# A linear-attention layer and six windowed transformer layers: v's projection moved within the slot, both sums of squares behind the division, mask matmuls on 32 rows

## The chip, the cores and the metric

The kernel runs on one core of one Trainium2 chip. The metric is the device time of one execution in microseconds (us). Before the change it is 3887.95 us, the median of three runs (3886.12 to 3890.18). In the text TensorE is the matrix engine (PE in the profile; PEld are its weight loads), VectorE is DVE, ScalarE is ACT, GpSimd is POOL, and SyncE (SP) issues the DMAs.

## What is computed

The input is 8 sequences of 512 tokens with 128 features. Two sublayers follow each other, each between two layer norms with a residual:

```
x = x + layernorm(linear_attention(layernorm(x)))
x = x + layernorm(stack(layernorm(x)))
```

The first is attention with a Taylor expansion of the exponential in place of the softmax. The second, where the change lies, is a stack of six layers. Each has local attention with 16 heads of 64 and a gated feed-forward part with GELU:

```
qkv = x @ Wqkv; q, k, v = split(qkv)             # x has half its features shifted by a token
q = l2norm(q) * qs;  k = l2norm(k) * ksc         # per head
q, k = rotary(q) * scale, rotary(k) / scale
sim  = q . k * 8     # a window of 32 queries sees 64 keys: its own window and the one before
sim  = where(mask, -big, sim);  attn = softmax(sim)
x = (attn @ v) @ Wo + x
x = (a * gelu(gate)) @ W2 + b2 + x,  [a, gate] = layernorm(shift(x)) @ W1 + b1
```

The mask of a window depends on places within the window alone: the same 32 x 64 pattern for each of the four windows of a block of 128 tokens, save the first window of a sequence, which has no window before it.

## The kernel before

The first sublayer runs by itself in the first 540 us or so. The stack then runs in *slots*, one turn of the loop at L703. A unit is one block of 128 tokens of one sequence in one layer; there are 6 x 8 x 4 = 192. They run through the loop as a pipeline: in slot t, `at(t, lag, step)` runs a step for unit t-lag. TensorE's order is written out by hand (`manual_schedule`, L694): it executes its instructions as the loop issues them. The other engines' orders come from a planner, which ranks instructions by a simulated time and by `high_priority`, and keeps to edges laid with `issue_behind`. Each engine executes in order.

In a slot TensorE's order is:

- `proj` 0 (unit t): q's projection, L421, four passes of 128x512 into PSUM tag "mm"
- `out_project` (t-3), L603, after which VectorE adds to `state` (L608)
- `proj` 1: k's projection
- `by_keys` (t-2): eight transposes of the exponentials into two banks of tag "tr", each emptied by ScalarE (L564, tile pT)
- `values` (t): v's projection, L481, into tag "mm"; ScalarE copies it to v0 (L482, in two banks at once); ten DMAs on SP (L489, L490, L492), or for the first block of a sequence eight and two memsets on GpSimd (L487), spread it by windows into v2
- `by_features` 0 (t-1): eight transposes of q and k, two banks of "tr", emptied by ScalarE (L514, tiles qT and kT)
- `weigh_values` (t-2), L574: 64x32 tiles of the array, into tag "s"; VectorE divides by the sums (L582, the division; tile on)
- `by_features` 4 (t-1): the other eight transposes, two banks of "tr"
- once in four slots each, for a whole sequence: `feed_norm` (transposes nx, L616), `feed_first` (transposes xn, L641), `feed_middle` (three chunks of L625 and L626 with GELU), `feed_last` (L657)
- `scores` (t-1): two mask matmuls (L527) start the two banks of "s" with the mask, and 64x32 tiles (L534) add the products; VectorE takes the maxima (L542), ScalarE the exponentials (L546)
- `out_by_features` (t-2): eight transposes, two banks of "tr", emptied by ScalarE (L596)

PSUM has eight banks, and all are used: "mm" has two buffers of two banks, "tr" two of one bank, "s" one of two banks. A buffer is written again when all who read its last tile are done. So the users of "mm" in a slot take turns: `proj` 0 and `values` have the same buffer, `proj` 1 the other, then the feed-forward steps.

In `proj`, VectorE multiplies the projection by the rotary tables (two L429, one L436), ScalarE squares it (two L444, tile sq), and GpSimd adds (L454). `sum_squares` is VectorE's reduction of sq (L457). For q (s=0) it is issued within `proj`; for k (s=1) after `weigh_values`, with an edge behind the last division. `unit_length` then makes the inverse root on ScalarE (L95, L97) and multiplies on GpSimd (L470). In slots with GELU it stands behind `feed_middle`, and ScalarE loads another activation table at the slot's start (L82) and back (L76).

Of the kernel before, what the change touches and what calls it, by code (L numbers as in the profile page):

```python
# [9 lines left out]
BF16 = mybir.dt.bfloat16  # L10
AF = mybir.ActivationFunctionType
ALU = mybir.AluOpType
AX = mybir.AxisListType
# [7 lines left out]
W = 32  # L21
NEG = -(2.0**100)
EPS = 1e-5


@with_exitstack
def sandwich_kernel(ctx: ExitStack, tc: tile.TileContext, ins: dict, out: bass.AP):
# [38 lines left out]
    mask = const.tile([P, 2 * W], BF16, tag="mask", name="mask")  # L66
    mask0 = const.tile([P, 2 * W], BF16, tag="mask0", name="mask0")

    def transposed(ps, src, rows, cols):
        nc.tensor.transpose(ps[:cols, :rows], src, ident[:rows, :rows])  # L70


    tables, exps, divisions = [], [], []

    def log_and_exp(behind):
        ld = nc.scalar.preload_act_table_set("natural_log_exp_and_others")  # L76
# [332 lines left out]
    def proj(u, s):  # L409

        L, b, j = u["L"], u["b"], u["j"]
        wqkv, tab = L["wqkv"], L["tab"]
        lhs = state[b][:, j * P : (j + 1) * P]
        if s == 0:
            u["ss"] = f2.tile([P, 2, H], F32, tag="ss", name="ss")
            u["qk"] = f2.tile([P, 2, H, 2, HF], F32, tag="qk", name="qk")
        ss, qk = u["ss"], u["qk"]

        ps = psum.tile([P, 2, H, HF], F32, tag="mm", name="mm")
        for a in range(2):  # L420
            nc.tensor.matmul(  # L421
                ps[:, a].rearrange("p h d -> p (h d)"), lhs, wqkv[:, s, a, :], start=True, stop=True
            )
        sq = f2.tile([P, H, 2, HF], F32, tag="sq", name="sq")
        t1 = f2.tile([P, 2, H, HF], F32, tag="t1", name="t1")
        t2 = f2.tile([P, 2, H, HF], F32, tag="t2", name="t2")

        def turned(a):
            nc.vector.tensor_tensor(  # L429
                t2[:, a], ps[:, 1 - a],  # L430
                tab[:, 2 * s + 1, j, HF * a : HF * (a + 1)].unsqueeze(1).to_broadcast([P, H, HF]),
                ALU.mult,
            )

        def straight():
            nc.vector.tensor_tensor(  # L436
                t1, ps,
                tab[:, 2 * s, j, :].rearrange("p (a d) -> p a d", a=2).unsqueeze(2)
                .to_broadcast([P, 2, H, HF]),
                ALU.mult,  # L440
            )

        def squared(a):
            nc.scalar.activation(sq[:, :, a, :], ps[:, a], AF.Square)  # L444

        turned(0)
        turned(1)
        straight()
        squared(0)
        squared(1)  # L450
        u["sq"] = sq
        if s == 0:
            sum_squares(u, 0)
        nc.gpsimd.tensor_tensor(qk[:, s].rearrange("p h a d -> p a h d"), t1, t2, ALU.add)  # L454

    def sum_squares(u, s):
        su = nc.vector.tensor_reduce(  # L457
            u["ss"][:, s], u["sq"].rearrange("p h a d -> p h (a d)"), AX.X, ALU.add
        )
        if s == 1 and divisions:  # L460
            issue_behind(su, divisions[-1])

    def unit_length(u):
# [10 lines left out]
    def values(u):  # L474
        L, b, j = u["L"], u["b"], u["j"]
        lhs = state[b][:, j * P : (j + 1) * P]

        v0 = f3.tile([P, 2, 512], F32, tag="v0", name="v0")
        ps = psum.tile([P, 2, 512], F32, tag="mm", name="mm")
        for p in range(2):  # L480
            nc.tensor.matmul(ps[:, p, :], lhs, L["wqkv"][:, 2, p, :], start=True, stop=True)  # L481
        nc.scalar.copy(v0, ps)  # L482

        v2 = f2.tile([P, 4, 512], F32, tag="v2", name="v2")
        for p in range(2):
            if j == 0:
                nc.gpsimd.memset(v2[HD * p : HD * p + W, 0, :], 0.0)  # L487
            else:
                nc.sync.dma_start(v2[HD * p : HD * p + W, 0, :], u["B"]["v0"][P - W : P, p, :])  # L489
            nc.sync.dma_start(v2[HD * p + W : HD * (p + 1), 0, :], v0[0:W, p, :])  # L490
            for w in range(1, 4):
                nc.sync.dma_start(  # L492
                    v2[HD * p : HD * (p + 1), w, :], v0[W * (w - 1) : W * (w + 1), p, :]
                )
        u["B"]["v0"] = v0
        u["v2"] = v2

    def by_features(u, c):

        j, qk, B_ = u["j"], u["qk"], u["B"]  # L500
        if c == 0:
            u["qT"] = f1.tile([P, NP, P], F32, tag="qT", name="qT")
            if j == 0:
                B_["kT"] = f2.tile([P, NP, W + P], F32, tag="kT", name="kT")
                nc.gpsimd.memset(B_["kT"][:, :, :W], 0.0)
            u["kT"] = B_["kT"]
        for s in range(2):
            ps = psum.tile([P, 4, P], F32, tag="tr", name="tr")
            for i in range(4):
                h0 = 2 * (c + i)  # L510
                transposed(ps[:, i, :], qk[:, s, h0 : h0 + 2].rearrange("p h a d -> p (h a d)"), P, P)
            dst = u["qT"][:, c : c + 4, :] if s == 0 else u["kT"][:, c : c + 4, W:]
            with tc.high_priority():
                nc.scalar.copy(dst, ps)  # L514
        if c == NP - 4 and j < NB - 1:
            B_["kT"] = f2.tile([P, NP, W + P], F32, tag="kT", name="kT")
            nc.gpsimd.tensor_copy(B_["kT"][:, :, :W], u["kT"][:, :, P:])

    def scores(u):

        qT, kT = u["qT"], u["kT"]


        mk = mask0 if u["j"] == 0 else mask
        sp = psum.tile([P, 2, NP, 2 * W], F32, tag="s", name="sp", bufs=1)
        for p in range(2):
            nc.tensor.matmul(  # L527
                sp[:, p], identb, mk.unsqueeze(1).to_broadcast([P, NP, 2 * W]),
                start=True, stop=False, skip_group_check=True,
            )  # L530
        for pair in range(NP):
            for w in range(4):
                for p in range(2):
                    nc.tensor.matmul(  # L534
                        sp[W * w : W * (w + 1), p, pair, :],
                        qT[HD * p : HD * (p + 1), pair, W * w : W * (w + 1)],
                        kT[HD * p : HD * (p + 1), pair, W * w : W * (w + 2)],
                        start=False, stop=True, skip_group_check=True,
                    )
        mx = f2.tile([P, 2, NP], F32, tag="mx", name="mx")  # L540
        with tc.high_priority():
            nc.vector.tensor_reduce(mx, sp, AX.X, ALU.max, negate=True)  # L542
        pe = f2.tile([P, NP, 2, 2 * W], F32, tag="pe", name="pe")
        for pair in range(NP):
            for p in range(2):
                ex = nc.scalar.activation(  # L546
                    pe[:, pair, p, :], sp[:, p, pair, :], AF.Exp, bias=mx[:, p, pair : pair + 1]
                )
                issue_behind(ex, tables[-1])
        exps.append(ex)  # L550
        su = f2.tile([P, NP, 2], F32, tag="su", name="su")
        nc.vector.tensor_reduce(su, pe, AX.X, ALU.add)
        nc.vector.reciprocal(su, su)
        u["pe"], u["su"] = pe, su
# [133 lines left out]
    def at(t, lag, step, *args, ends=False):  # L688
        if 0 <= t - lag < len(units) and (not ends or units[t - lag]["j"] == NB - 1):
            step(units[t - lag], *args)  # L690
# [3 lines left out]
    with tc.manual_schedule(engines={mybir.EngineType.PE}):  # L694
# [8 lines left out]
        for t in range(len(units) + 7):  # L703
            if t < len(units):
                u = units[t]
                if u["l"] not in layers:
                    layers[u["l"]] = load_layer(u["l"])
                u["L"] = layers[u["l"]]


            gelus = 0 <= t - 5 < len(units) and units[t - 5]["j"] == NB - 1
            if gelus:
                gelu_only()
            at(t, 0, proj, 0)
            at(t, 3, out_project)
            at(t, 0, proj, 1)
            at(t, 2, by_keys)

            if t == 0:
                head_norm(NG - 1)  # L720
            at(t, 0, values)
            if t == 1:
                attn_out(B - 1)
            if t == 3:
                to_state(B - 1)
            at(t, 1, by_features, 0)
            at(t, 2, weigh_values)
            at(t, 0, sum_squares, 1)
            if not gelus:
                at(t, 0, unit_length)  # L730
            at(t, 1, by_features, 4)
            at(t, 3, feed_norm, ends=True)
            at(t, 4, feed_first, ends=True)
            at(t, 5, feed_middle, ends=True)
            if gelus:
                at(t, 0, unit_length)
            at(t, 6, feed_last, ends=True)
            at(t, 1, scores)
            at(t, 2, out_by_features)

# [90 lines left out]
```

## Time and profile before

The profile is of one execution of 3893.85 us, whose span from first to last instruction is 3892.1 us; TensorE's granted clock was 0.99 of full speed in it.

| | |
|---|---|
| median of three runs | 3887.95 us |
| profiled execution | 3893.85 us, span 3892.1 us |
| slots 1503.63 to 1520.32, to 1535.01, to 1551.53, to 1571.3 us | 16.69, 14.69, 16.52, 19.8 us |
| TensorE busy between 1000 and 2000 us | 969.0 us |
| the same for VectorE, ScalarE, GpSimd | 763.6, 714.2, 554.4 us |
| data moved | 233.46 MB, mean 60 GB/s |

How to read it: a line of the groups names the source line, the engine, the operation, output and inputs by the program's tiles, the shape, and the count; after the bar come busy time in us and the mean of one in ns; after the second bar the engine's idle time just before these instructions, and who ended it. In the timeline the columns are start and length in us, then engine, line, operation; instructions of one kind in a row are merged, with their count. Matmuls are pipelined: lengths overlap, and the time that a step takes is the distance from its start to the next one's start. An f32 matmul appears as two passes, a transpose as one.

### The profile page before, as it was taken

To read this page: it belongs to the slowest core of one execution; us is meant where nothing else is said; L and a number is where in the kernel's file an instruction comes from. 1 tells how busy PE (TensorE), PEld (TensorE's weight loads), DVE (VectorE), ACT (ScalarE), POOL (GpSimd) and SP (SyncE) were. 2 spreads that over 40 slices of the span, in tenths; PEclk is the share of its full clock that TensorE was granted. 3 is DMA by queue.
4 is the path that set the end of the run, shared out by engine and by line. 5 is a ranking of instruction groups with operands and counts; after the bars stand their busy time and mean duration, and the time that the engine had idled before them with its cause. 6 is when DMAs were issued, how large, how long until landed. Compare 5 with 4: busy or idle time off the path is not lost.

```text
span 3892.1 us, 149565 instructions
## 1 busy us (share of the span) xinstructions
PE 3729.8 (96%) x65600; PEld 2474.2 (64%) x65600; DVE 2818.2 (72%) x4300; ACT 2657.5 (68%) x6745; POOL 1837.0 (47%) x1311
## 2 busy tenths in 40 slices
PE   8999989999999999999999999999999999999997
PEld 4555456666666666666666666666666666666665
DVE  4555567777867777777777777777787777777775
ACT  5565656776767777777777677777677777766664
POOL 0000025555555555555555555555555555555552
PEclk9999999999999999999999999999999999999998
DMA  2000012222222222222222322223222222222221
GB/s 81 17 9 12 6 50 71 59 66 60 76 74 63 63 63 66 71 75 65 60 62 64 82 65 66 65 56 82 70 66 59 66 65 56 65 68 68 64 67 37
DMA packets 153208, 233.46 MB, mean 60 GB/s; under 512 B 32622, under 2 KB 53356, under 8 KB 151788
## 3 DMA queue, kind: packets, MB, share of 16 engines
q1 hardware_dynamic: 152556, 223.89, 22.4%
q8 instruction: 517, 8.47, 0.9%
q14 instruction: 135, 1.11, 0.1%
HBM read 24.54 MB, written 4.19 MB: 7 GB/s over the span
## 4 chain that ended last, share of the span: by engine, by line
PE 89%; ACT 5%; issue 3%; DVE 2%; DMA 0%; POOL 0%; POOLq 0%; DVEq 0%; SPq 0%; ACTq 0%
PE tr L70 17%; PE mm L421 17%; PE mm L481 9%; PE py L603 9%; PE sp L534 7%; PE po L574 6%; PE y L282 4%; PE mm L625 3%; PE py L657 3%; PE mm L626 3%; PE sc L252 2%; PE sp L527 2%; ACT sq L444 2%; PE vv L230 2%; PE po L318 2%
## 5 line engine op out<-in xcount | busy, mean ns | idle before, releaser
L454 POOL TENSOR_TENSOR qk<-t,t 128x1024 f32<-128x1024 f32 x384 | 909.2, 2368 | 999.6 <-DVE t L436 999.5
L421 PE MATMUL mm<-wqkv,state 128*128 128x512 f32 x1536 | 727.1, 596 | 3.7 <-ACT v L482 2.6
L470 POOL TENSOR_TENSOR qk<-qk,ss 128x1024 f32<-128x1024 f32 x384 | 722.3, 1902 | 16.0
L429 DVE TENSOR_TENSOR t<-mm,tab 128x512 f32<-128x512 f32 x768 | 497.8, 685 | 242.8 <-PE mm L421 231.3
L546 ACT ACTIVATE pe<-sp,mx 128x64 f32<-128x64 f32 x3072 | 651.4, 376 | 27.6 <-DVE mx L542 27.3
L436 DVE TENSOR_TENSOR t<-mm,tab 128x1024 f32<-128x1024 f32 x384 | 465.9, 1213 | 0.0
L457 DVE TENSOR_REDUCE ss<-sq 128x16 f32<-128x1024 f32 x384 | 461.9, 1203 | 2.0 <-ACT sq L444 2.0
L444 ACT ACTIVATE sq<-mm 128x512 f32<-128x512 f32 x768 | 422.6, 610 | 47.2 <-DVE t L436 45.6
L603 PEld LDWEIGHTS py<-oT,wo 128*128 128x128 f32 x3072 | 374.8, 193 | 93.5 <-issue 56.2
L70 PEld LDWEIGHTS tr<-ident,qk 128*128 128x128 f32 x3072 | 345.7, 141 | 127.1 <-issue 105.7
L70 PE MATMUL tr<-ident,qk 128*128 128x128 f32 x3072 | 412.1, 277 | 7.4 <-ACT qT L514 2.3
L596 ACT COPY oT<-tr 128x512 f32<-128x512 f32 x384 | 207.3, 589 | 266.2 <-PE tr L70 265.2
L421 PEld LDWEIGHTS mm<-wqkv,state 128*128 128x128 f32 x1536 | 264.1, 192 | 191.6 <-issue 188.0
L481 PE MATMUL mm<-wqkv,state 128*128 128x512 f32 x768 | 367.9, 602 | 16.8 <-ACT sq L444 16.8
L603 PE MATMUL py<-oT,wo 128*128 128x128 f32 x3072 | 376.0, 276 | 1.0 <-ACT oT L596 0.9
L582 DVE TENSOR_TENSOR on<-po,su 128x1024 f32<-128x1024 f32 x192 | 235.1, 1224 | 170.1 <-PE po L574 170.1
L534 PEld LDWEIGHTS sp<-kT,qT 64*32 64x32 f32 x24576 | 271.9, 106 | 116.7 <-issue 113.8
L574 PE MATMUL po<-v,pT 64*32 64x64 f32 x24576 | 299.3, 225 | 44.7 <-issue 44.7
L482 ACT COPY v<-mm 128x1024 f32<-128x1024 f32 x192 | 194.5, 1013 | 211.0 <-PE mm L481 211.0
L534 PE MATMUL sp<-kT,qT 64*32 64x64 f32 x24576 | 312.2, 227 | 26.0 <-issue 25.2
L574 PEld LDWEIGHTS po<-v,pT 64*32 64x32 f32 x24576 | 258.5, 105 | 86.4 <-issue 86.2
L542 DVE TENSOR_REDUCE mx<-sp 128x16 f32<-128x1024 f32 x192 | 234.6, 1222 | 106.9 <-PE sp L534 106.3
(108 smaller groups left out, 5171.0 us busy)
## 6 DMA issues: line engine op xcount, KB each, us to landing
v<-v SPq DMA_DIRECT2D x1152, 128.0 KB
v<-v SPq DMA_DIRECT2D x672, 64.0 KB
wqkv<-in_L_ffn_Wqkv_dram SPq DMA_DIRECT2D x6, 1536.0 KB
wo<-in_L_ffn_Wo_dram SPq DMA_DIRECT2D x6, 512.0 KB
xin<-_attn_hidden_states_dram SPq DMA_DIRECT2D x8, 256.0 KB
xr<-_attn_hidden_states_dram SPq DMA_DIRECT2D x8, 256.0 KB
x<-xr SPq DMA_DIRECT2D x8, 256.0 KB
xr<-x SPq DMA_DIRECT2D x8, 256.0 KB
```

Source lines behind the costliest of these rows:

```text
L70: nc.tensor.transpose(ps[:cols, :rows], src, ident[:rows, :rows])
L421: nc.tensor.matmul(ps[:, a].rearrange("p h d -> p (h d)"), lhs, wqkv[:, s, a, :], start=True, stop=True)
L429: nc.vector.tensor_tensor(t2[:, a], ps[:, 1 - a], tab[:, 2 * s + 1, j, HF * a : HF * (a + 1)].unsqueeze(1).to_broadcast([P, H, HF]), ALU.mult,
L436: nc.vector.tensor_tensor(t1, ps, tab[:, 2 * s, j, :].rearrange("p (a d) -> p a d", a=2).unsqueeze(2) .to_broadcast([P, 2, H, HF]), ALU.mult,)
L444: nc.scalar.activation(sq[:, :, a, :], ps[:, a], AF.Square)
L454: nc.gpsimd.tensor_tensor(qk[:, s].rearrange("p h a d -> p a h d"), t1, t2, ALU.add)
L470: nc.gpsimd.tensor_tensor(t, t, ss[:, i, :].unsqueeze(2).to_broadcast([P, H, HD]), ALU.mult)
L481: nc.tensor.matmul(ps[:, p, :], lhs, L["wqkv"][:, 2, p, :], start=True, stop=True)
L534: nc.tensor.matmul(sp[W * w : W * (w + 1), p, pair, :], qT[HD * p : HD * (p + 1), pair, W * w : W * (w + 1)], kT[HD * p : HD * (p + 1), pa ...
L546: ex = nc.scalar.activation(pe[:, pair, p, :], sp[:, p, pair, :], AF.Exp, bias=mx[:, p, pair : pair + 1])
L574: nc.tensor.matmul(po[W * w : W * (w + 1), p, pair, :], pT[r, pair, W * w : W * (w + 1)], v2[r, w, HD * pair : HD * (pair + 1)], start=Tru ...
L603: nc.tensor.matmul(py, L["wo"][:, c, :], oT[:, c, :], start=(c == 0), stop=(c == NP - 1))
```

## The change

Four things change.

1. `values` is split. Its matmuls stay in `values`, which moves from before `by_features` 0 to after `weigh_values`. The copy of v and all that follows it, the DMAs and memsets of v2 too, become `spread`, called after `by_features` 4, with an edge that puts the copy behind the last copy of q's and k's transposes.
2. q's sum of squares leaves `proj` and is issued beside k's, after `weigh_values`; both have the edge behind the last division. The tile sq is kept for each.
3. The mask matmuls of all blocks but a sequence's first take 32 rows: the stationary operand is a new constant `each` (64 x 128, four 32 x 32 identities side by side in each half), the moving one the mask's first 32 rows for p=0 and the next 32 for p=1. The first block of a sequence keeps the 128-row identity and `mask0`.
4. `each` is made once, at the start, by eight small casts on VectorE.

```diff
+    each = const.tile([2 * W, P], BF16, tag="each", name="each")
+    for a in range(2):
+        for w in range(4):
+            nc.vector.tensor_copy(
+                each[W * a : W * (a + 1), W * w : W * (w + 1)], ident[W * a : W * (a + 1), W * a : W * (a + 1)]
+            )
...
-        u["sq"] = sq
-        if s == 0:
-            sum_squares(u, 0)
+        u["sq", s] = sq
...
-            u["ss"][:, s], u["sq"].rearrange("p h a d -> p h (a d)"), AX.X, ALU.add
+            u["ss"][:, s], u["sq", s].rearrange("p h a d -> p h (a d)"), AX.X, ALU.add
         )
-        if s == 1 and divisions:
+        if divisions:
             issue_behind(su, divisions[-1])
...
             nc.tensor.matmul(ps[:, p, :], lhs, L["wqkv"][:, 2, p, :], start=True, stop=True)
-        nc.scalar.copy(v0, ps)
+        u["v0"], u["v0ps"] = v0, ps
+
+    def spread(u):
+        j, v0 = u["j"], u["v0"]
+        cp = nc.scalar.copy(v0, u.pop("v0ps"))
+        if copies:
+            issue_behind(cp, copies[-1])
...
-                nc.scalar.copy(dst, ps)
+                copies.append(nc.scalar.copy(dst, ps))
...
-        mk = mask0 if u["j"] == 0 else mask
...
         for p in range(2):
+            r = slice(W * p, W * (p + 1))
+            lhs, mk = (identb, mask0) if u["j"] == 0 else (each[r], mask[r])
             nc.tensor.matmul(
-                sp[:, p], identb, mk.unsqueeze(1).to_broadcast([P, NP, 2 * W]),
+                sp[:, p], lhs, mk.unsqueeze(1).to_broadcast([lhs.shape[0], NP, 2 * W]),
                 start=True, stop=False, skip_group_check=True,
             )
...
+            at(t, 1, by_features, 0)
+            at(t, 2, weigh_values)
             at(t, 0, values)
...
-            at(t, 1, by_features, 0)
-            at(t, 2, weigh_values)
+            at(t, 0, sum_squares, 0)
             at(t, 0, sum_squares, 1)
             if not gelus:
                 at(t, 0, unit_length)
             at(t, 1, by_features, 4)
+            at(t, 0, spread)
```

More of the change, by code (lines that the diff above doesn't have):

```diff
@@ L67, in sandwich_kernel @@
     mask0 = const.tile([P, 2 * W], BF16, tag="mask0", name="mask0")
+    each = const.tile([2 * W, P], BF16, tag="each", name="each")
[4 more added lines that the diff above has]
+            )
     def transposed(ps, src, rows, cols):
         nc.tensor.transpose(ps[:cols, :rows], src, ident[:rows, :rows])
-    tables, exps, divisions = [], [], []
+    tables, exps, divisions, copies = [], [], [], []
     def log_and_exp(behind):
```

## The prediction

> **What bounds the kernel now.** I read the busy shares, then the chain of waits, the groups by line and shape, and the timeline of single instructions on TensorE and ScalarE.
>
> ```profile
> PE 3729.8 (96%) x65600; PEld 2474.2 (64%) x65600; DVE 2818.2 (72%) x4300; ACT 2657.5 (68%) x6745; POOL 1837.0 (47%) x1311
> PE 89%; ACT 5%; issue 3%; DVE 2%; DMA 0%; POOL 0%; POOLq 0%; DVEq 0%; SPq 0%; ACTq 0%
> L481 PE MATMUL mm<-wqkv,state 128*128 128x512 f32 x768 | 367.9, 602 | 16.8 <-ACT sq L444 16.8
> L70 PE MATMUL tr<-ident,xn 128*128 128x128 f32 x192 | 32.2, 290 | 14.4 <-ACT qT L514 11.9 <-DVE xn L115 2.5
> L574 PE MATMUL po<-v,pT 64*32 64x64 f32 x24576 | 299.3, 225 | 44.7 <-issue 44.7
> ```
>
> TensorE is the limit: what it doesn't wait for costs nothing. The change can save 16.8 us of visible waiting before v's projection (L481). The second TensorE row is a wait that two transposing steps in a row already pay. The third is instruction supply, which stops long runs of small matmuls.
>
> Now one slot (one block of 128 tokens through the loop at L703; 192 of them). Columns: start, length, engine, line.
>
> ```profile
> 1525.54 1.04 PE L70 MATMUL tr<-ident,pe 128*128 128x128 f32 x8
> 1526.18 1.08 ACT L564 COPY pT<-tr 128x512 f32<-128x512 f32 x2 [0.27 <-PE tr L70]
> 1526.41 1.88 PE L481 MATMUL mm<-wqkv,state 128*128 128x512 f32 x4
> 1528.13 1.04 PE L70 MATMUL tr<-ident,qk 128*128 128x128 f32 x8
> 1529.10 1.48 PE L574 MATMUL po<-v,pT 64*32 64x64 f32 x128
> 1530.52 1.09 PE L70 MATMUL tr<-ident,qk 128*128 128x128 f32 x8
> 1531.45 0.60 PE L70 MATMUL nx<-ident,state 128*128 128x128 f32 x4
> 1531.90 0.59 PE L527 MATMUL sp<-mask,identb 128*128 128x512 bf16 x2
> ```
>
> Read from start to start, for the lengths overlap. Eight transposes (two PSUM banks of tag "tr", which has just two) take 0.87 us, v's projection 1.72, and nothing lies between. The two copies that empty the banks run 1526.18 to 1527.26, **under v's projection**. That cover is what the change takes away.
>
> **The price of the lost cover.** After it, by_features(0) follows by_keys at once, and its first bank is by_keys' first. The trace has this case once in four slots: feed_first after by_features(4).
>
> ```profile
> 1546.75 1.09 PE L70 MATMUL tr<-ident,qk 128*128 128x128 f32 x8
> 1547.45 0.58 ACT L514 COPY qT<-tr 128x512 f32<-128x512 f32 x1 [1.37 <-PE tr L70]
> 1547.93 0.59 ACT L514 COPY kT<-tr 128x512 f32<-128x512 f32 x1
> 1548.09 0.66 PE L70 MATMUL tr<-ident,xn 128*128 128x128 f32 x4 [0.24 <-ACT qT L514]
> 1548.58 0.59 PE L527 MATMUL sp<-mask,identb 128*128 128x512 bf16 x2
> ```
>
> From 1546.75 to 1548.09 it takes 1.34 us where by_features(4) takes 0.93 (1530.52 to 1531.45): 0.41 to 0.42 us of waiting, and xn's four transposes take 0.49 instead of nx's 0.45 (the next weights weren't loaded ahead; single starts say 0.055). So **0.475 us**. The copies themselves say the same: by_keys starts at 0, its first copy at 0.64 and ends at 1.23, with 0.06 to the next matmul 1.29, against 0.87. The second copy ends at 1.72, when the first bank has just been refilled (1.29+0.055+0.436=1.78), so the second bank adds nothing to 0.05. In the 144 slots without GELU: 144 x 0.475 = 68.4 us.
>
> In the 48 slots with GELU the table load makes the squares late, and v waits:
>
> ```profile
> 1556.76 1.04 PE L70 MATMUL tr<-ident,pe 128*128 128x128 f32 x8
> 1556.96 1.09 ACT L444 ACTIVATE sq<-mm 128x512 f32<-128x512 f32 x2
> 1557.93 1.08 ACT L564 COPY pT<-tr 128x512 f32<-128x512 f32 x2
> 1558.10 1.98 PE L481 MATMUL mm<-wqkv,state 128*128 128x512 f32 x4 [0.31 <-ACT sq L444]
> ```
>
> by_keys ends at 1557.63. v now waits 0.47 us and loses 0.10 of weight load (1.82 instead of 1.72): 0.57, which goes. In its place by_features(0) waits for the first pT copy, 1558.52+0.06, so 0.95, plus 0.055: 1.01. Net +0.44, x 48 = 21 us. **The wait saved is smaller than the wait that takes its place.** Together +89 us; bounds 0.42 x 192 = 81 and 0.53 x 192 = 102.
>
> **v's projection after the small tiles.** A step that follows another tiling of the array can't load its first weights ahead.
>
> ```profile
> 310.54 1.98 PE L303 MATMUL ms<-ysq,same 128*128 128x512 f32 x4
> 312.45 1.51 PE L282 MATMUL y<-am,tv 128*64 128x384 f32 x8
> ```
>
> Four f32 matmuls between two other tilings take 1.91 us against v's 1.72: 0.19, of which 0.09 is the exit (transposes before L574 take 0.97 against 0.87), so 0.10 the entry; transposes there pay 0.06 (0.93 against 0.87). by_features(4) is freed of 0.06, v pays 0.10: +0.046 x 192 = +9 us (0 to 20).
>
> **Mask matmuls.** Two bf16 matmuls, 0.216 us each by their starts, in 144 slots (blocks with j=0 keep the full identity). On rows 0-31 and 32-63 they may run together, as L252's four row groups do (sixteen passes of 256 columns in 0.87 us, as long as four). But 128 to 32 rows is one more change of tiling: 0.09, and the first weights exposed: 0.10 for loads that last 192 ns, 0.06 for 141 ns, so about 0.02 for L527's 98 ns, an estimate from these rows. The later change to 64x32 is paid already. 0.216-0.007-0.09-0.02 = 0.10, x 144 = **-14 us**. Bounds: -31 (no change paid) and +16 (no overlap, change paid). The Trainium skill, "TensorEngine Tiling (Array Packing)", Key Properties, says that a change of tiling mode drains the engine; "TensorE: Matmul & The Clock Gate", Part 3, has packed matmuls start some 4 ns apart. By the second page alone this part would save 31 us; the 0.09 us rows side with the first.
>
> **v's copy behind q's and k's.** ScalarE's copy (1.01 us) moves to after by_features(4): from its start S, qT and kT copies run to S+1.72, v's to S+2.73. The bank pair is wanted again by feed_middle's second chunk in GELU slots, at S+0.87+1.72=S+2.59; with 0.06 it starts at 2.79: +0.2, some of it taken back at the third chunk: 0.17 x 48 = **+8 us** (0 to 12). Elsewhere the pair's next user comes over 4 us after S. Queued behind the copy on ScalarE: GELU (ready S+2.8), unit_length, the exponentials (S+3.5 or later). The ten DMAs on SP and the memset on GpSimd of v2 start some 3 us later; v2 is read two slots on, some 25 us away, and SP spent 7 to 8 us on them.
>
> **Sums of squares behind the division.** Both reductions (1.20 us each) now queue after L582. k's rotation comes 1.2 us sooner; the division needs L574, which ends 1.2 us sooner too. From the slot's start (1520.32 for the one shown) the sums end at 12.65 us today (1532.97); then at 8.96 (end of L574: 6.09 for by_keys, 0.4 wait, 1.0, 1.4) + 0.2 + 1.22 + 2 x 1.2 = 12.8. The mask waits for the division alone, which now has v's 1.72 us as cover, but it waited only 0.6 us in all. Behind them on VectorE: layer norm, then the score maxima, ready later still. 0 us; if the maxima slipped by 1 us in the slots with layer norm, the exponentials have some 0.7 us of slack (end 1539.92, wanted by the second bank at 1540.67), so 0.3 x 48 = 14. Eight small casts for `each` at the start lie in VectorE's idle 3.4 us before x lands: 0 (at most 1.5).
>
> **Instruction supply.** Blocks of L574 and L534 take 1.41 us at best; over that they add 58 and 52 us in all, mostly stops for instructions. The new order shifts where a fetch falls: v's 1.72 us leaves the stretch before L574 and enters the one before L534. 0, with -30 to +30.
>
> **Sum.** 89+9-14+8 = +92 us. The profiled execution took 3893.85 us (span 3892.1), 5.9 over the median: 3887.95+92 = **3980 us**.
>
> **The rivals.**
> 1. *Faster: the banks come free in time.* If by_keys' copies kept pace with its transposes, so that by_features(0) didn't wait, the wait of v would simply go: -0.57 x 48 = -27, with -14+9+8 -24, so 3864. It decides if the first copy ends within 0.87 us of by_keys' start; today 1.23. For it: ScalarE is 68% busy; against: it idles before this copy, so it can't be earlier. Chance 0.09 (0.07 below -0.2%, 0.02 within).
> 2. *Supply gets worse.* L574 is reached 1.72-0.475 us sooner while the fetch comes when it did: 62 stops grow by up to 1.25: +78, so 4058. Against: in the records of the instruction queue these fetches start about 0.5 us before L574, whatever went before. 0.08.
> 3. *The mask doesn't overlap* (the change doesn't do what it says): +16 for -14, so 4010. Against: L252. 0.11.
> 4. *ScalarE puts pT's copies ahead of the squares in GELU slots:* their 0.57 us stays saved, -27, so 3953. 0.12.
>
> The forecast keeps 0.60. Range 3930 to 4030: it takes in 3, 4 and the bounds of supply, and leaves 1 and 2 out (0.17). Faster by over 0.2% (about what this measurement tells from none) 0.07, same 0.02, slower 0.91.
>
> **What would show it.** TensorE's transposes of qk with an idle time of tens of us put down to ScalarE's pT copy (today none), by_keys to by_features(0) 1.29 us from start to start; L481's wait for sq gone, its block 1.82; L527 to L534 0.42 instead of 0.52; L625 with a wait for v's copy. If by_keys to by_features(0) stays 0.87, the prediction falls.

## The result, and the profile after

The changed kernel takes **4027.03 us** (median; 4021.14 to 4030.63), beside 3889.06 us for the kernel before (3886.12 to 3890.41): a ratio of **1.0354, with a 95% interval from 1.0336 to 1.0372**. It is slower by 138 us; the forecast was slower by 92, with the range up to 4030. The profiled execution took 4021.14 us with a span of 4019.4 us at a granted clock of 0.989.

The busy shares, the engines of the chain of waits, then five TensorE groups by line and shape, and last the two groups of the kernel before (transposes of q and k, scores) that weren't shown yet:

```profile
PE 3758.1 (93%) x65600; PEld 2464.0 (61%) x65600; DVE 2815.7 (70%) x4308; ACT 2666.0 (66%) x6745; POOL 1840.5 (46%) x1311
PE 78%; ACT 9%; DVE 5%; issue 4%; POOL 2%; DMA 1%; SPq 0%; ACTq 0%; POOLq 0%; DVEq 0%
```

```profile
L76 PE MATMUL tr<-ident,qk 128*128 128x128 f32 x3072 | 419.8, 278 | 102.9 <-ACT pT L576 82.6 <-POOL qk L458 18.6 <-ACT qT L524 1.4
...
L485 PE MATMUL mm<-wqkv,state 128*128 128x512 f32 x768 | 391.8, 632 | 6.5 <-issue 4.9 <-ACT sq L450 1.4
...
L546 PE MATMUL sp<-kT,qT 64*32 64x64 f32 x24576 | 304.8, 226 | 12.2 <-issue 12.1
...
L586 PE MATMUL po<-v,pT 64*32 64x64 f32 x24576 | 295.3, 226 | 75.6 <-issue 75.6
...
L76 PE MATMUL tr<-ident,xn 128*128 128x128 f32 x192 | 32.3, 289 | 13.5 <-ACT qT L524 11.0 <-DVE xn L121 2.5
```

```profile
L70 PE MATMUL tr<-ident,qk 128*128 128x128 f32 x3072 | 412.1, 277 | 7.4 <-ACT qT L514 2.3 <-issue 2.2 <-ACT pT L564 1.2
...
L534 PE MATMUL sp<-kT,qT 64*32 64x64 f32 x24576 | 312.2, 227 | 26.0 <-issue 25.2
```

TensorE's busy time rose by 28 us, and it went from 96% of the span to 93%: most of the loss is waiting. The transposes of q and k waited 7.4 us before and now wait 102.9: 82.6 of it is put down to ScalarE's copy of pT, 18.6 to GpSimd's qk (wrongly, where it was looked at; see the slots with `feed_first`). v's projection (L485, L481 before) lost its 16.8 us of waiting for the squares, but its busy time rose by 24 us. The idle time "issue" of the weighing matmuls (L586, L574 before) rose from 44.7 to 75.6 us, that of the scores (L546, L534 before) fell from 26.0 to 12.2. xn's transposes wait as they did.

One slot without GELU, from the timeline (start, length, engine, line):

```profile
1627.26 1.04 PE L76 MATMUL tr<-ident,pe 128*128 128x128 f32 x8
...
1627.90 1.08 ACT L576 COPY pT<-tr 128x512 f32<-128x512 f32 x2 [0.27 <-PE tr L76]
...
1628.63 1.12 PE L76 MATMUL tr<-ident,qk 128*128 128x128 f32 x8 [0.33 <-ACT pT L576]
1629.68 1.48 PE L586 MATMUL po<-v,pT 64*32 64x64 f32 x128
1631.09 1.98 PE L485 MATMUL mm<-wqkv,state 128*128 128x512 f32 x4
```

From 1627.26 to 1628.63 `by_keys` takes 1.37 us where it took 0.87: the first pT copy (0.586 us) ends at 1628.49, and `by_features` 0 starts 0.144 us behind it. That block takes 1.05 us (0.97 before). The projection of v comes straight after the small tiles.

From the single starts I took, for 45 slots of each of the four kinds (with `feed_norm`, `feed_first`, `feed_middle`, `feed_last`), the mean distance from each step's start to the next. A slot went from 17.164 to 17.879 us; times 192 that is 137 us, as much as the medians differ. (The two profiled executions differ by 127 us in their spans: outside the slots where all steps run, the changed kernel's was some 9 us shorter.)

| step, start to next start | before, us | after, us | difference x 192 |
|---|---|---|---|
| `by_keys` | 0.984 | 1.569 | +112 |
| `by_features` 0 | 0.967 | 1.050 | +16 |
| v's projection | 1.746 | 1.892 (half of the slots at 1.821) | +28, of which +14 without stops |
| `weigh_values` | 1.719 | 1.877 | +30 |
| `by_features` 4 (with what it waits in `feed_first`) | 1.042 | 0.989 | -10 |
| masks, and what the step ahead of them pays | | | -17 |
| `feed_middle`, second chunk | | | +5 |
| `scores` | 1.685 | 1.575 | -21 |
| `out_by_features`, `proj` 0 | 2.737 | 2.701 | -7 |

### The profile page after: what moved, and what is told of

The parts are those of the page before. It is cut to its first block, busy times and chain, and to the rows that moved or that the text cites. A ratio compares the mean times of both kernels' runs of the same rounds, so it can differ in the third digit from the quotient of the medians.

```text
span 4019.4 us, 149714 instructions
## 1 busy us (share of the span) xinstructions
PE 3758.1 (93%) x65600; PEld 2464.0 (61%) x65600; DVE 2815.7 (70%) x4308; ACT 2666.0 (66%) x6745; POOL 1840.5 (46%) x1311
## 4 chain that ended last, share of the span: by engine, by line
PE 78%; ACT 9%; DVE 5%; issue 4%; POOL 2%; DMA 1%; SPq 0%; ACTq 0%; POOLq 0%; DVEq 0%
PE tr L76 15%; PE mm L427 13%; PE mm L485 9%; PE po L586 7%; PE py L615 7%; PE sp L546 6%; PE y L288 4%; PE mm L637 3%; PE mm L638 3%; PE py L669 3%; PE sc L258 2%; ACT pT L576 2%; POOL qk L458 2%; ACT sq L450 2%; PE vv L236 2%
## 5 line engine op out<-in xcount | busy, mean ns | idle before, releaser
L427 PE MATMUL mm<-wqkv,state 128*128 128x512 f32 x1536 | 728.5, 598 | 2.9 <-ACT v L490 2.6
L524 ACT COPY qT<-tr 128x512 f32<-128x512 f32 x384 | 224.8, 585 | 509.3 <-PE tr L76 504.8
L76 PE MATMUL tr<-ident,qk 128*128 128x128 f32 x3072 | 419.8, 278 | 102.9 <-ACT pT L576 82.6
L461 DVE TENSOR_REDUCE ss<-sq 128x16 f32<-128x1024 f32 x384 | 448.5, 1209 | 0.7 <-ACT sq L450 0.6
L485 PE MATMUL mm<-wqkv,state 128*128 128x512 f32 x768 | 391.8, 632 | 6.5 <-issue 4.9
L586 PE MATMUL po<-v,pT 64*32 64x64 f32 x24576 | 295.3, 226 | 75.6 <-issue 75.6
L586 PEld LDWEIGHTS po<-v,pT 64*32 64x32 f32 x24576 | 257.4, 105 | 108.4 <-issue 107.9
L546 PE MATMUL sp<-kT,qT 64*32 64x64 f32 x24576 | 304.8, 226 | 12.2 <-issue 12.1
L546 PEld LDWEIGHTS sp<-kT,qT 64*32 64x32 f32 x24576 | 269.6, 105 | 68.2 <-issue 66.4
```

The source lines that it names most:

```text
L427: nc.tensor.matmul(ps[:, a].rearrange("p h d -> p (h d)"), lhs, wqkv[:, s, a, :], start=True, stop=True)
L546: nc.tensor.matmul(sp[W * w : W * (w + 1), p, pair, :], qT[HD * p : HD * (p + 1), pair, W * w : W * (w + 1)], kT[HD * p : HD * (p + 1), pa ...
L586: nc.tensor.matmul(po[W * w : W * (w + 1), p, pair, :], pT[r, pair, W * w : W * (w + 1)], v2[r, w, HD * pair : HD * (pair + 1)], start=Tru ...
```

## The experiments

The theory: v's projection covered the two pT copies, and without that cover `by_features` 0 waits for its bank. Rival A: the other parts (sums, copy, masks) cost the time. Rival B: the supply of instructions does. Each ratio is to the kernel before, timed on the same chip (median there 3898.15 to 3905.7 us). The runs went to four chips, so ratios of two runs are told apart only where their intervals are. Steps and idle times are compared with the one trace of the kernel before, an execution of 3893.85 us, 4 to 12 us below these medians, so a sum of steps can come out that much higher than the ratio.

### The move alone, and the change without it

The kernel before with v's whole step behind `weigh_values`:

```diff
+            at(t, 1, by_features, 0)
+            at(t, 2, weigh_values)
             at(t, 0, values)
...
-            at(t, 1, by_features, 0)
-            at(t, 2, weigh_values)
```

> The kernel before, with v's projection (its copy and DMAs with it) moved behind weigh_values and nothing else. Theory 'cover' (by_features 0 waits for by_keys' two PSUM banks): by_keys to by_features 0 takes 1.37 us from start to start in slots without GELU and 1.9 with it, as in the changed kernel, and the time is 4030 us (4005 to 4055), since the mask's 16 us aren't saved and v's early copy stands ahead of q's and k's second pair. Rival 'sums' (VectorE's order with both reductions behind the division delays the maxima and all that follows): within 20 us of the kernel before. Rival 'late copy' (v's copy and its DMAs being late): within 20 us of the kernel before.

Measured: 4052.07 us, ratio 1.0384 (1.037 to 1.0398).

The changed kernel with that move undone, all else kept:

```diff
             at(t, 0, values)
...
+            at(t, 1, by_features, 0)
+            at(t, 2, weigh_values)
             at(t, 0, sum_squares, 0)
```

> The changed kernel with v's matmuls put back between by_keys and by_features 0; copy late, sums behind the division and 32-row mask stay. Theory 'cover': the 136 us go, 3889 - 16 (mask) + 5 (feed_middle waits for v's copy) + 12 (squares late in slots after a layer norm) = 3890 us (3875 to 3905). Rival 'sums' and rival 'late copy': stays at 4000 us or more.

Measured: 3909.36 us, ratio 1.0023 (1.0014 to 1.0032).

The move alone costs at least as much as the whole change (the intervals just touch), and all the rest costs 0.2% (in it v waits 26.3 us for the squares in slots with GELU, 16.8 before). Two groups of the move alone:

```profile
L70 PE MATMUL tr<-ident,qk 128*128 128x128 f32 x3072 | 419.6, 278 | 95.5 <-ACT pT L564 89.9 <-POOL qk L470 2.8 <-ACT qT L514 1.8
L70 PE MATMUL tr<-ident,xn 128*128 128x128 f32 x192 | 32.3, 289 | 33.7 <-ACT qT L514 31.3 <-DVE xn L115 2.5
```

The first row is the wait of the changed kernel. The second, 14.4 us in the kernel before, is the price of v's copy left in `values`: ScalarE does it ahead of the qT copy, and in slots with `feed_first` `by_features` 4 takes 1.74 us (1.36 before, 1.30 after the full change). So the late copy, forecast as a loss of 8 us, takes back 0.44 x 48 = 21 us here. Rival A falls as the main cause.

### The other parts, each alone

The kernel before with q's sum behind the division:

```diff
-        if s == 0:
-            sum_squares(u, 0)
...
+            at(t, 0, sum_squares, 0)
             at(t, 0, sum_squares, 1)
```

> The kernel before with q's sum of squares behind the division. Theory 'cover' gives it a small part: in slots after one with layer norm the maxima come 0.4 us later, so the exponentials, so q's squares; v's matmuls wait some 0.25 us there: +12 us, 3901 (3889 to 3910). Rival 'sums': +60 us or more.

Measured: 3902.63 us, ratio 0.9999 (0.9991 to 1.0008). The expected 12 us aren't there.

With the masks of 32 rows alone (the constant `each`, and the lines of `scores` as in the change):

> The kernel before with the 32-row mask matmuls alone. Theory: two row groups run together, one change of tiling is added: 0.11 us a slot in 144 slots, -16 us, 3873 (3865 to 3880). Rival without a price for the change of tiling: -31 us, 3858. Rival without overlap: +15 us, 3904.

Measured: 3891.02 us, ratio 0.997 (0.9961 to 0.9979): 10.6 us instead of 16. Its steps show why. In a slot with `feed_norm` the mask block goes from 0.522 to 0.318 us and nx's transposes ahead of it from 0.455 to 0.533, as forecast; but the scores behind it go from 1.807 to 1.966 us. They are reached sooner, and stop longer for instructions. How much of the 0.16 us is due to that isn't sharply shown: two kernels without these masks, the load alone and the late copy alone (below), have 1.92 and 1.90 us there.

With v's copy behind the copies of q and k alone:

```diff
-        nc.scalar.copy(v0, ps)
+        u["v0"], u["v0ps"] = v0, ps
...
             at(t, 1, by_features, 4)
+            at(t, 0, spread)
```

> The kernel before with v's copy and its DMAs issued behind q's and k's second copies, all else as before. From the run with v put back (+8 us with the mask's -11 and the sums' 0 in it) this part is left with +18 us: feed_middle's second chunk waits some 0.1 us for the copy in GELU slots (+5), and the scores there take 1.67 instead of 1.42 us, while v's DMAs run (+12): 0.45% slower (0.3 to 0.6). Rival 'copy is free' (the predicted +8 and nothing in the scores): 0.2%.

Measured: 3910.8 us, ratio 1.0016 (1.0005 to 1.0026), less than expected. The scores in slots with GELU did go from 1.416 to 1.618 us, as expected. Of idle time, the weighing matmuls' fell from 44.7 to 41.2 us, but the scores' rose from 26.0 to 29.3, so what makes the time fall short of the expected 18 us stays open.

The changed kernel with q's sum back in `proj`:

```diff
+        if s == 0:
+            sum_squares(u, 0)
...
-            at(t, 0, sum_squares, 0)
```

> The changed kernel with q's sum of squares back in proj. Alone, this part measured nothing; together with the lost cover it should: in slots after a layer norm q's squares end 0.4 us later and push pT's copies, for which by_features 0 now waits (1.64 instead of 1.37 us). Theory: 13 us and some of the GELU slots' wait come back, 12 to 20 us below the changed kernel, ratio to before 1.031 (1.029 to 1.033), and by_keys to by_features 0 is 1.37 in these slots. Rival 'sums are free in any company': 1.0354 as the changed kernel.

Measured: 4033.99 us, ratio 1.0338 (1.0322 to 1.0354): no clear difference from the changed kernel's 1.0354, so the moved sum is worth little in either.

### Half of the cover

The changed kernel with v's first matmul between `by_keys` and `by_features` 0, the second behind `weigh_values`:

```diff
+            at(t, 0, values, 0)
             at(t, 1, by_features, 0)
             at(t, 2, weigh_values)
-            at(t, 0, values)
+            at(t, 0, values, 1)
```

> The changed kernel with v's first matmul (0.86 us) between by_keys and by_features 0 and the second behind weigh_values. Theory 'cover': 0.86 us is more than the wait of 0.49, so the wait goes as a whole and not by half, and by_features 0 takes 0.97 again; left are the late copy, the first weights behind weigh_values (+9) and some of the instruction supply (0 to 15), less the mask: ratio 1.006 (1.003 to 1.010). Rival 'it is the place of v itself, behind the small tiles' (supply and first weights): about half of the loss stays, 1.018.

Measured: 3922.5 us, ratio 1.0053 (1.0041 to 1.0066). Three groups of it:

```profile
L76 PE MATMUL tr<-ident,qk 128*128 128x128 f32 x3072 | 410.0, 277 | 6.4 <-issue 3.6 <-ACT qT L523 1.4 <-ACT pT L575 1.2
L485 PE MATMUL mm<-wqkv,state 128*128 128x512 f32 x768 | 430.2, 642 | 21.0 <-ACT sq L450 17.1 <-issue 3.9
L585 PE MATMUL po<-v,pT 64*32 64x64 f32 x24576 | 295.6, 225 | 78.8 <-issue 78.8
```

Half of v's projection (0.86 us) covers the wait of 0.49 us **whole**: 82.6 us put down to pT became 1.2. Half of the cover hid all of the wait, not half of it. The wait for the squares is back in slots with GELU.

### The same wait, with v in another place

Rival B needs a kernel with the wait but another order of long and short instructions. Here `values` and `by_features` 0 of the kernel before change places, and v stays ahead of `weigh_values`:

```diff
+            at(t, 1, by_features, 0)
             at(t, 0, values)
...
-            at(t, 1, by_features, 0)
             at(t, 2, weigh_values)
```

> The kernel before with v's projection and by_features 0 exchanged: by_keys, by_features 0, values, weigh_values. The cover is gone, but v stays ahead of the small tiles, so instruction supply and first weights are as before. Theory 'cover': 0.49 us of wait in 144 slots and 0.59 in 48 (99 us), 0.08 for weights loaded late in by_features 0 (15), 5 less for v: +109 us, ratio 1.028 (1.025 to 1.031), against 1.038 for the move alone; L574 then stops for some 45 us, as before. Rival 'place behind the small tiles': 1.01 or less.

Measured: 3969.24 us, ratio 1.0171 (1.0157 to 1.0185), some 43 us less than expected. Two of its groups, and then the weighing row of the move alone:

```profile
L70 PE MATMUL tr<-ident,qk 128*128 128x128 f32 x3072 | 427.3, 281 | 91.4 <-ACT pT L564 87.4 <-POOL qk L470 2.8 <-ACT qT L514 0.7
L574 PE MATMUL po<-v,pT 64*32 64x64 f32 x24576 | 298.3, 226 | 12.8 <-issue 11.1
```

```profile
L574 PE MATMUL po<-v,pT 64*32 64x64 f32 x24576 | 295.8, 226 | 79.6 <-issue 79.6
```

The wait is the theory's to 0.01 us (`by_keys` 1.367 in most slots, 1.913 in the typical one with GELU). But the weighing matmuls are idle for 12.8 us, not 79.6, and not the 45 that were expected. By the steps' means, 0.356 us x 192 = 68 us of the difference of 83 us between these two kernels lies in `weigh_values`; the scores give 31 back, and the rest is `by_features` 0, which in the move alone pays for standing ahead of the small tiles (+19), v's own stops (+16) and `by_features` 4 (+13). **The order of long passes and bursts of small matmuls has a price of its own.** A stop in the changed kernel, and then one in this kernel:

```profile
1574.30 1.30 PE L586 MATMUL po<-v,pT 64*32 64x64 f32 x107
1577.57 0.42 PE L586 MATMUL po<-v,pT 64*32 64x64 f32 x21 [1.96 <-issue]
```

```profile
1566.63 1.44 PE L574 MATMUL po<-v,pT 64*32 64x64 f32 x123
1568.53 0.31 PE L574 MATMUL po<-v,pT 64*32 64x64 f32 x5 [0.46 <-issue]
```

In the DMA records, the queue that carries instructions has 517 transfers of 16 KB; the 131,200 matmuls and weight loads make one for some 254 of them (with the engine's waits, 256), and the stops lie 256 instructions apart or a multiple of that. Where a weighing block stops, the last such transfer began (medians) 0.51 us ahead of the block in the kernel before, 1.06 us ahead here, and 0.66 us *behind* the block's start in the changed kernel (0.67 in the move alone). The later it begins, the longer the block is idle: 0.29 us here, 0.65 in the kernel before, 1.8 and 1.9 in those two.

### Why the slots with `feed_first` wait longer

In them `by_keys` takes 1.64 us, against 1.37 in those with `feed_norm` and `feed_last`. The timeline of the changed kernel there, and VectorE just before it:

```profile
1571.44 1.20 ACT L450 ACTIVATE sq<-mm 128x512 f32<-128x512 f32 x2
...
1571.57 1.04 PE L76 MATMUL tr<-ident,pe 128*128 128x128 f32 x8
...
1572.39 1.21 ACT L576 COPY pT<-tr 128x512 f32<-128x512 f32 x2
...
1573.25 1.12 PE L76 MATMUL tr<-ident,qk 128*128 128x128 f32 x8 [0.65 <-POOL qk L458]
```

```profile
1565.75 1.36 DVE L121 TENSOR_SCALAR xn<-nx,ln_mv,ln_rs 128x128 f32<-128x128 f32 x4 [0.63 <-ACT ln_rs L103]
1567.03 1.22 DVE L554 TENSOR_REDUCE mx<-sp 128x16 f32<-128x1024 f32 x1
```

VectorE in such a slot of the kernel before:

```profile
1534.65 0.73 DVE L115 TENSOR_SCALAR xn<-nx,ln_mv,ln_rs 128x128 f32<-128x128 f32 x2 [0.60 <-ACT ln_rs L97]
1535.30 1.21 DVE L542 TENSOR_REDUCE mx<-sp 128x16 f32<-128x1024 f32 x1
```

The profile puts this wait down to GpSimd, but `by_features` 0 starts 0.144 us behind the end of the first pT copy (1573.11), as in the other slots. The squares still run when `by_keys` has its first bank full, and the pT copy comes behind them. They are late because the exponentials are, and those wait for the score maxima (mx), which VectorE does behind all four subtractions of the layer norm (xn); in the kernel before mx stood behind two of them and began 0.45 us sooner (1.10 us behind the scores' end, where it is now 1.55). The changed kernel with the subtractions put behind mx:

```diff
-            nc.vector.tensor_reduce(mx, sp, AX.X, ALU.max, negate=True)
+            first = nc.vector.tensor_reduce(mx, sp, AX.X, ALU.max, negate=True)
+        while late:
+            issue_behind(late.pop(), first)
...
-        layer_norm(f2, xn, ps, NB, by_log=True)
+        late.extend(layer_norm(f2, xn, ps, NB, by_log=True))
```

> The changed kernel with the last step of feed_norm's layer norm (four subtractions) queued behind the score maxima of the same slot on VectorE. Theory 'late maxima': in the slot after a layer norm q's squares end at 5.8 and not 6.3 us, by_keys to by_features 0 takes 1.37 and not 1.64 us: -13 us, ratio 1.032 (1.030 to 1.034). Rival: the time comes back as another wait: 1.0354.

Measured: 4027.47 us beside 3902.88, ratio 1.0309 (1.0289 to 1.033). `by_keys` in these slots is back at 1.367 us, and VectorE's order is the intended one:

```profile
1578.00 1.22 DVE L556 TENSOR_REDUCE mx<-sp 128x16 f32<-128x1024 f32 x1 [0.41 <-PE sp L548]
1579.14 1.35 DVE L121 TENSOR_SCALAR xn<-nx,ln_mv,ln_rs 128x128 f32<-128x128 f32 x4
```

So the late maxima cost `by_keys` 13 us. Putting q's sum back changed this little (1.57 us): it was the order on VectorE, not the sum. Whether the kernel gains the 13 us is not shown. The ratio lies just below the changed kernel's interval, but only since the kernel before took 3902.88 us beside it and not 3889.06; the times themselves are alike (4027.47 and 4027.03 us), and in its trace a slot takes 17.88 us as in the changed kernel's: v's projection and the weighing matmuls stop for longer (80.1 us idle in weighing, where it was 75.6). So the rival, that the time comes back as another wait, stands.

### What beats both kernels

The slots with GELU lose time in `by_keys` in both kernels (1.31 us instead of 0.87 in the kernel before), since the table load stands ahead of the squares and of the pT copy. Here it is issued behind the pT copies:

```diff
-        issue_behind(ld, exps[-1])
+        issue_behind(ld, ready[-1])
...
-                nc.scalar.copy(pT[:, c : c + 4, :], ps)
+                ready.append(nc.scalar.copy(pT[:, c : c + 4, :], ps))
...
-            if gelus:
-                gelu_only()
             at(t, 0, proj, 0)
...
             at(t, 2, by_keys)
+            if gelus:
+                gelu_only()
```

First by itself in the kernel before:

> The kernel before with the GELU table's load behind pT's copies alone. Theory: v's 0.57 us go in 48 GELU slots, -27 us; by the pair with the mask (-28 in all, mask -11) -17 to -27: ratio 0.995 (0.993 to 0.9965).

Measured: 3876.64 us, ratio 0.9937 (0.9925 to 0.9949).

Then with the masks of 32 rows:

> The kernel before with the 32-row mask and, in GELU slots, ScalarE's load of the GELU table issued behind pT's copies and not at the slot's start. Theory: q's squares then end in time, v's 0.57 us of waiting goes in 48 slots (-27 us), with the mask's -11: -38 us, ratio 0.990 (0.988 to 0.993), by_keys to v 0.87 us in GELU slots. Rival: the load delays the copies or GELU later by as much as it saves: 0.997, as with the mask alone.

Measured: **3872.71 us, ratio 0.9929 (0.9916 to 0.9943)**, the fastest, though its interval overlaps that of the load alone. ScalarE's timeline in a slot with GELU, and the groups of v's projection and of the scores:

```profile
1627.17 1.08 ACT L572 COPY pT<-tr 128x512 f32<-128x512 f32 x2 [0.27 <-PE tr L77]
1628.26 1.28 ACT L89 ACT_TABLE_LOAD   x1
1629.56 1.01 ACT L489 COPY v<-mm 128x1024 f32<-128x1024 f32 x1
```

```profile
L488 PE MATMUL mm<-wqkv,state 128*128 128x512 f32 x768 | 363.8, 596 | 2.2 <-ACT sq L451 2.2
L542 PE MATMUL sp<-kT,qT 64*32 64x64 f32 x24576 | 316.3, 226 | 37.0 <-issue 36.0
```

v's wait of 16.8 us falls to 2.2 without moving v: `by_keys` takes 0.873 us in every kind of slot. The masks' share is again partly given back: the scores' idle time is 37.0 us, 30.6 with the load alone and 26.0 in the kernel before. The 0.9929 lies at the upper end of what was expected.

Last, that kernel with v cut in two, the second matmul between `by_features` 0 and `weigh_values`, in the hope that a long pass just ahead of the burst shortens its stops, as in the exchanged order:

```diff
-            at(t, 0, values)
+            at(t, 0, values, 0)
...
             at(t, 1, by_features, 0)
+            at(t, 0, values, 1)
             at(t, 2, weigh_values)
```

> The kernel before with the 32-row mask, the GELU table's load behind pT's copies, and v's projection cut in two: the first matmul (0.86 us) between by_keys and by_features 0, the second between by_features 0 and weigh_values. Theory: 0.86 us covers the wait of 0.49, and four long passes right before L574 (two matmuls would be eight minutes of nothing; here one f32 matmul, two passes of 0.43 us) let the next instructions be fetched earlier: fetches start some 0.9 us before L574 instead of 0.5, L574's idle time falls from 47 to about 30 us, ratio 0.988 (0.985 to 0.991). Rival: supply depends on nothing that lies right before L574: 0.993, as without the cut.

A bracket in it is a slip; what is meant is that one f32 matmul is two passes of 0.43 us. Measured: 3880.42 us, ratio 0.9945 (0.9931 to 0.9958): no gain. The transfers still begin 0.45 us ahead of the block, and it stops no less than without the cut (47.3 us):

```profile
L584 PE MATMUL po<-v,pT 64*32 64x64 f32 x24576 | 298.9, 225 | 52.7 <-issue 52.7
```

What of the order makes a fetch early or late stays open.

## Why the prediction was right, and where its sizes were off

The mechanism was right: the bank that `by_features` 0 shares with `by_keys` is the new wait, it is larger than the wait that it replaces, and the move alone, its undoing, the half and the exchange all show it. That the time fell within the range is in part luck: 4027 lies 3 us inside its upper end. The range was that wide for the bounds of supply and for rivals 3 and 4; the wait went past its own bounds of 81 to 102, with 112+16-5 = 123 us. Term by term, in us:

| term of the sum | predicted | measured |
|---|---|---|
| `by_keys` to the next start, less v's old wait | +83 | +112 |
| first weights of `by_features` 0 | +11 | +16 |
| v's first weights behind the small tiles | +14 | +14 |
| `by_features` 4 freed of that | -11 | -10 |
| masks with 32 rows | -14 | -17 |
| v's late copy before the second chunk | +8 | +5 |
| sums of squares, maxima | 0 | in the first row |
| instruction supply and the rest (weighing +30, v +14, scores -21, others -7) | 0 | +16 |

(The text's +89 is the first two rows less v's 0.10 in the slots with GELU; its +9 is the next two over all slots. The scores' -21 holds +11 that are not stops: those of the slots with GELU, see the last section.)

**The wait.** The step that was mis-sized is "with 0.06 to the next matmul 1.29". Behind the pT copy it was 0.144 us (0.143 to 0.146 in nine of ten slots, in the move alone and the exchanged order too): 1.37 instead of 1.29, and 1.91 instead of 1.82 with GELU; some 0.08 x 192 = 15 us. The 0.06 came from the one place of the trace that had the case, a qT copy ahead of xn's transposes, and there it is 0.054 us in the changed kernel too. The trace shows what stands between. In each of 188 slots of the changed kernel, TensorE's weight-load queue has an instruction that only waits (EVENT_SEMAPHORE) between the pT copy's end and the first weights of q's and k's transposes, which wait for two engines (the bank from ScalarE, qk from GpSimd). In the slot shown it begins 0.04 us behind the copy, lasts 0.05, and the first matmul follows 0.06 later. Ahead of xn's transposes, which wait for one engine, there is none in any of 46 slots. No run took it away, so that it is the cause is not proved. The second bank waits the same way, 0.144 us behind the second copy: that costs 0.05 us, the upper end of "the second bank adds nothing to 0.05", of which the sum took nothing; the first weights cost 0.03 instead of 0.055, together the 16 us of the second row. The other 14 us of the first row are the late maxima (13) and v's old wait, on average 0.44 instead of 0.47 us.

**The maxima.** "Behind them on VectorE: layer norm, then the score maxima, ready later still. 0 us" failed. They stood in the middle of the layer norm's subtractions and came behind them; that is nearly the bound of 14 us that the same paragraph names. It counted the slack up to the second bank's need, but once the cover is gone `by_features` 0 wants ScalarE's pT copy at once, and that stands behind the squares. The sums themselves cost nothing (0.9999 alone).

**v behind the small tiles.** 1.82 us in the typical slot, and `by_features` 4 at 0.873: as worked out. The reading that a step behind another tiling has its first weights exposed held to 0.01 us.

**The masks.** From L527's start to L534's 0.42 us were foreseen; the block takes 0.318 and the step ahead of it 0.08 to 0.10 more. The two matmuls start 3 to 4 ns apart where it was 216, so the pair overlaps, and the 0.08 to 0.10 us are read as the price of the change of tiling. The third rival, that they don't overlap, falls. The Trainium skill, "TensorEngine Tiling (Array Packing)", Key Properties, says that a change of tiling mode drains the engine; the 0.08 to 0.10 us agree.

**The late copy.** As foreseen, with a wait before the second chunk (the weight load of L637), from the timeline:

```profile
1597.27 1.03 ACT L490 COPY v<-mm 128x1024 f32<-128x1024 f32 x1
...
1597.41 1.02 PE L638 MATMUL mm<-xnT,w 128*128 128x512 f32 x2
...
1598.36 0.30 PEld L637 LDWEIGHTS mm<-xnT,w 128*128 128x128 f32 x2 [0.75 <-ACT v L490]
1598.36 1.13 PE L637 MATMUL mm<-xnT,w 128*128 128x512 f32 x2
```

Two starts of L638 and L637 lie 0.95 us apart instead of 0.86. Together with the move, the same edit earned 21 us elsewhere (see the move alone), which the forecast had built in without seeing that it did.

**Supply.** The argument against the second rival, "in the records of the instruction queue these fetches start about 0.5 us before L574, whatever went before", was wrong: they start from 1.06 us before to 0.67 after it, by what stands ahead. The rival was right in kind, since blocks of L586 stop for longer (42 stops of over 0.3 us, the middle one 1.8 us, where there were 62 with 0.65), but the scores stop for less, and the net is +16 us, not +78.

**The other rivals.** The first (banks free in time) falls: by_keys' first copy ends 1.22 us from its start, not within 0.87. The fourth falls too; in the slots with GELU ScalarE still does the squares first, so their delay passes on to the bank:

```profile
1588.39 1.28 ACT L88 ACT_TABLE_LOAD   x1
...
1589.69 1.08 ACT L450 ACTIVATE sq<-mm 128x512 f32<-128x512 f32 x2
...
1590.66 1.08 ACT L576 COPY pT<-tr 128x512 f32<-128x512 f32 x2
...
1591.40 1.12 PE L76 MATMUL tr<-ident,qk 128*128 128x128 f32 x8 [0.88 <-ACT pT L576]
```

## What to carry to other kernels

Before a step is moved on the engine that sets the end, ask what it covers where it stands: here 0.86 us of other work between two users of the same two PSUM banks hid a wait of 0.49 us whole, and without it `by_keys` took 112 us longer in all. The Trainium skill, "Perfetto Trace Analysis", Optimizing Tensor Performance, asks that groups of matmuls rotate through banks so that emptying one overlaps the next group; this case agrees and adds a length: with 1.37 us from a bank's first write to the next, two banks that are filled in 0.87 us are too few, unless other work covers the 0.49 us between (here 0.86 us of it did). Where the step waits for another engine, move that engine's late work (here a table load, -0.6%) rather than the step.

## What the runs showed of the hardware

- The supply of instructions depends on the order of work. The same burst of 128 small matmuls, in 192 slots, was idle, nearly always for "issue", 12.8 us with v's long passes just ahead of it, 44.7 with transposes between, 75.6 with v behind it. One long f32 matmul of the two just ahead of it did not do it (52.7). Time saved just ahead of a burst seems to be partly lost in it: the masks' 16 us became 10.6.
- In slots with GELU the scores take 1.62 to 1.65 us instead of 1.42 wherever v's copy is late and its DMAs run during them (the changed kernel, its version with v back, the copy alone), without one long stop; with the copy early they take 1.42 us even where v is moved. This was only seen to go together; its cause wasn't tried, and the transfers by themselves don't fit: in the move alone 208 KB were moved during these scores (252 in the changed kernel, 78 in the kernel before) and they took 1.42 us.
- From the end of ScalarE's copy to the first TensorE write of the freed bank it took 0.054 us behind the qT copy and 0.144 us behind the pT copy, alike in nearly every slot of five kernels. Behind the pT copy a separate wait instruction stands in between, behind the qT copy none.
